# Dividing attention outputs two steps later in a fused attention and expert kernel

## The chip, the cores and the metric

The kernel runs on one core of a Trainium2 chip. The metric is device time in microseconds (us) of one execution. The engines are TensorE (PE, whose weight loads the profile counts apart as PEld), VectorE (DVE), ScalarE (ACT), GpSimd (POOL) and SyncE (SP), which here only issues DMA transfers. Every engine works through its own queue in order.

## The reference, cut to what matters

The input x is 8 batches of 1024 tokens with 256 features, in float32. A transformer block is computed: self-attention with 16 heads of 16 features, a relative position bias that is multiplied by a gate per query, then a residual and a layernorm, then a mixture of 8 experts (two per token, capacity 2560 rows, a fallback network for what overflows), again with a residual and a layernorm. What matters for the change is the attention:

```python
gate_out = gate_a * (gate_b * gru_const - 1.0) + 2.0
gated_bias = gate_out * pos_bias[None]
scores = jnp.einsum('bhid,bhjd->bhij', q, k) * scale + gated_bias
attn = jax.nn.softmax(scores, axis=-1)
out = jnp.einsum('bhij,bhjd->bhid', attn, v)
```

The kernel does not normalise `attn`. It multiplies exp(scores) by v with a column of ones added to it, so that the sum of each softmax row comes out as one more row of the output, and divides the output by that sum afterwards. This division is what the change moves.

## The kernel before, in words

**Units and steps.** The attention is cut into 64 units: 8 batches times 8 pairs of heads (HP = 2). A unit is 16 steps (STEPS): 8 tiles j of 128 keys times 2 chunks c of 512 queries, step s = 2j + c. The loop at L1309 counts steps as g, with unit u and step s of it; `sb` is the step within a batch's 128. In this document the place of a unit is u mod 8, its place in its batch. The order of work is written out by hand (`manual_schedule`, L393): what is recorded first stands first in its engine's queue.

**One step.** PE multiplies keys and queries of two heads into the PSUM tile `sc` (L1107, two buffers). DVE adds the gated bias `gb` (L1122, in 12 of 16 steps), ACT takes the exponential into `pr` (L1129), and in odd steps PE multiplies four `pr` tiles with v into `o_acc` (L1137). Interleaved with it, 21 steps ahead (LEAD), an upper bound of each query's scores is found: two PE products `pm` (L1023, L1027), a relu on ACT (L1052) and a fold on DVE (L1064). `pm0` has one PSUM bank; in even steps the product takes the common bank instead, if that is free. Before a unit begins, `shift` (L1075) turns these bounds into a row of its queries: a PE transpose `pmr` at step 11 (SHIFT_AT), a copy on ACT (L1083), a DVE operation (L1085), and two DMAs `qs<-row` (L1092), which the first scores of the next unit read.

**POOL** makes the gated bias of a tile every second step (`gate_biases`, L983, two tiles ahead, four buffers, from `bias` and `gates`), a diagonal `dgb` (L996), and the small operations of the streams.

**The end of a unit.** `take_outputs` (L1146) works in the steps of the next unit: ACT copies `o_acc` into `osb` at step 1 (L1149); at step 2 four DMAs take the rows of sums to 128 partitions (`sums<-osb`, L1154); at step 4 DVE takes reciprocals (L1170); at step 5 four DMAs take them back (`recs<-sums`, L1164). Then `divide` (L1173), at step DIVIDE_AT: PE spreads the reciprocals over the partitions (`pb<-recs,sel`, L1177, two matmul records), in the step after it DVE multiplies `osb` by `pb` (L1181), and four DMAs store it (`oD<-osb`, L1191). `sums`, `recs` and `osb` have one buffer each.

**SP's queue in a unit.** Step 1: two loads of `biasb`. 2: four `sums`. 3 and 4: twelve loads of `ks` and `ks_d` for the unit after next. 5: four `recs`. 6: seven loads of `qs`. 8: `bias`. 9: `gates` of the next unit's tiles 0 to 2 (L965). Then four `oD`. 13: two `qs<-row`. 15: the other `gates`. Among them, up to about unit 23, stands every fourth step one transfer that clears `xd` or `yd` (L402).

**Streams.** What a batch's neighbours need runs beside the steps as generators: the prologue (projections) of the next batch, the epilogue (output projection `po`, layernorm, routing) of the batch before, and then 16 scatters of rows (`xd<-xt`, L888) on POOL, one in each odd step. All of them, and `divide` and `shift`, share one PSUM bank (`ps_x`). A user of it is held to its last read (HELD: read by ACT, SLOW: read by DVE, a step later); `Streams.bank` gives the bank to the list `own` (`divide`, `shift`) first, then to the streams in turn. In step 10, the step ahead of the shift, streams get no bank (`others`, L1356). The streams of a batch begin at `sb == 12`, in its first unit; the epilogue reads `oD`, which the last division of the batch before has to have stored.

After the units come the epilogue of the last batch and the expert stage (L1378 to L1565), which the diff does not touch.

## Time and profile before

| what | value |
|---|---|
| median of 3 runs | 3706.02 us (3704.2 to 3713.74) |
| the profiled execution's own time | 3705.5 us |
| its span | 3703.8 us |
| PE busy | 3293.6 us (89%) |
| PEld busy | 1663.7 us (45%) |
| POOL busy | 2221.0 us (60%) |
| ACT busy | 2045.0 us (55%) |
| DVE busy | 1944.0 us (52%) |
| first scores of unit 0, last scores of unit 63 | 147.7 us, 2522.0 us from the span's start |
| mean unit of batches 1 to 6, places 0 to 7 | 35.9, 44.4, 41.4, 43.6, 38.6, 32.9, 33.2, 33.2 us |

The busy shares are means over the whole span, expert stage included. The last row is read from the starts of the scores' matmuls (L1107): units at places 1 to 3 carry most of the streams' PE work, units at places 4 to 7 and 0 little of it.

### The profile page before, as it was taken

How to read it: one execution, taken by the hardware profiler on the slowest of the kernel's cores; microseconds unless marked ns; L12 is line 12 of the kernel's file. 1: busy time of each engine (PE TensorE's matmuls, PEld its weight loads, DVE VectorE, ACT ScalarE, POOL GpSimd, SP SyncE). 2: the span in 40 equal slices, each digit the busy share in tenths (PEclk: the TensorE clock that was granted, in tenths of full speed). 3: DMA queues.
4: the chain of work that ended last, by engine and by line, in shares of the span. 5: the costliest groups of instructions: out<-in, count | busy, mean ns of one | idle time of the engine just before them, and what ended most of it. 6: DMA issues, size and time to landing. Idle time of an engine off the chain costs nothing. (4 is left out here: it accounts for less than half of the span.)

```text
span 3703.8 us, 53431 instructions
## 1 busy us (share of the span) xinstructions
PE 3293.6 (89%) x16263; PEld 1663.7 (45%) x16263; DVE 1944.0 (52%) x5559; ACT 2045.0 (55%) x3084; POOL 2221.0 (60%) x2619
## 2 busy tenths in 40 slices
PE   4798898999899999999999999995299999999998
PEld 2242243334334334334333433332176667677776
DVE  2455566665756656665666576662033444344443
ACT  1576776777767777777777777772022222222222
POOL 2566666876886787787787688683333333333332
PEclk8899999999999999999999999996599999999999
DMA  5566666565543444444434444430322321332220
GB/s 133 153 167 192 167 172 183 173 195 181 179 140 110 144 135 122 134 136 122 139 123 141 133 123 128 129 111 15 107 70 74 90 87 54 92 94 94 71 89 22
DMA packets 380594, 455.71 MB, mean 123 GB/s; under 512 B 87653, under 2 KB 285410, under 8 KB 380282
## 3 DMA queue, kind: packets, MB, share of 16 engines
q1 hardware_dynamic: 338602, 388.06, 35.5%
q0 software_dynamic: 19296, 43.38, 4.1%
q10 hardware_dynamic: 22384, 20.58, 1.9%
q8 instruction: 138, 2.26, 0.3%
q14 instruction: 174, 1.43, 0.1%
HBM read 315.16 MB, written 140.54 MB: 123 GB/s over the span
## 5 line engine op out<-in xcount | busy, mean ns | idle before, releaser
L1129 ACT ACTIVATE pr<-sc 128x1024 f32<-128x1024 f32 x1024 | 1046.8, 1023 | 303.7 <-DVE sc L1122 297.9
L983 POOL TENSOR_TENSOR gb<-bias,gates 128x1024 f32<-128x1024 f32 (+2 forms) x512 | 1070.5, 2091 | 190.1 <-DMA gates<-gd 114.3
L1064 DVE CUSTOM_DVE_ANT_0 over<-pm,over 128x512 f32<-128x512 f32 x1024 | 704.3, 688 | 884.7 <-ACT over L1052 281.3
L1052 ACT ACTIVATE over<-pm 128x512 f32<-128x512 f32 x1024 | 609.3, 595 | 344.0 <-PE pm L1027 327.2
L1107 PE MATMUL sc<-qs,ks 122*128 122x512 bf16 x2048 | 625.1, 386 | 26.3 <-ACT pr L1129 18.5
L1122 DVE TENSOR_TENSOR sc<-sc,gb 128x640 f32<-128x640 f32 (+3 forms) x768 | 599.6, 781 | 46.6 <-POOL gb L983 21.0
L1027 PE MATMUL pm<-biasb,dgb 128*128 128x320 bf16 (+2 forms) x2048 | 581.7, 284 | 17.2 <-POOL dgb L996 17.2
L1137 PE MATMUL o_acc<-pr,v 128*17 128x512 f32 x4096 | 562.5, 621 | 0.3 <-ACT pr L1129 0.3
L1474 PE MATMUL ph<-xsT,w 128*128 128x512 f32 (+1 forms) x1440 | 487.6, 497 | 13.0 <-ACT xsT L1414 13.0
L1489 PE MATMUL py<-w,hT 128*128 128x256 f32 x2208 | 485.0, 379 | 5.9 <-DVE ys L1496 5.9
L1489 PEld LDWEIGHTS py<-w,hT 128*128 128x128 f32 x2208 | 419.2, 190 | 74.5 <-issue 10.5
L1023 PE MATMUL pm<-ks,qs 120*128 120x512 bf16 x1024 | 397.8, 388 | 57.3 <-DVE mh L1064 33.9
L1023 PE MATMUL pm<-ks_d,qs 120*128 120x512 bf16 x1024 | 397.1, 388 | 25.0 <-ACT over L1052 13.6
L1023 PEld LDWEIGHTS <-qs 120*128 120x128 bf16 x2048 | 208.9, 102 | 467.4 <-issue 303.4
L1481 ACT ACTIVATE hT<-ph,b_sb 128x512 f32<-128x512 f32 (+1 forms) x360 | 211.6, 588 | 287.3 <-PE ph L1474 286.3
L1474 PEld LDWEIGHTS ph<-xsT,w 128*128 128x128 f32 x1440 | 270.2, 190 | 212.7 <-issue 166.5
L1414 ACT COPY xsT<-pt 128x512 f32<-128x512 f32 (+1 forms) x90 | 39.5, 489 | 566.9 <-PE pt L1411 472.8
L143 POOL TENSOR_TENSOR rs<-rstd,neghalf 128x1 f32<-128x1 f32 x138 | 78.2, 566 | 442.2 <-DVE rstd L141 441.8
L1027 PEld LDWEIGHTS <-dgb 128*128 128x128 bf16 x2048 | 202.4, 99 | 301.6 <-issue 161.8
L996 POOL TENSOR_TENSOR dgb<-anti,grev 128x256 bf16<-128x256 f32 x512 | 314.2, 614 | 4.6
L1107 PEld LDWEIGHTS <-ks 122*128 122x128 bf16 x2048 | 199.8, 100 | 202.0 <-issue 52.3
L419 POOL TENSOR_TENSOR parts<-rest,parts 128x512 bf16<-128x512 f32 (+1 forms) x80 | 92.6, 1158 | 267.0 <-ACT parts L418 201.6
(184 smaller groups left out, 2929.7 us busy)
## 6 DMA issues: line engine op xcount, KB each, us to landing
gates<-gd SPq DMA_DIRECT2D x64, 832.0 KB
biasb<-stripb SPq DMA_DIRECT2D x128, 288.0 KB
gates<-gd SPq DMA_DIRECT2D x64, 576.0 KB
bias<-blocks SPq DMA_DIRECT2D x64, 512.0 KB
xd<-zero SPq DMA_DIRECT2D x51, 522.0 KB
ks<-kd SPq DMA_DIRECT2D x384, 64.0 KB
qs<-qd SPq DMA_DIRECT2D x384, 64.0 KB
yd<-zero SPq DMA_DIRECT2D x40, 512.0 KB
```

What stands on the lines that cost most here:

```text
L983: nc.gpsimd.tensor_tensor(gb_[:, :, off : off + hi - lo], me.bias[:, :, off : off + hi - lo], gates[:, :, lo - at : hi - at], ALU.mult,)
L996: nc.gpsimd.tensor_tensor(dg, anti.unsqueeze(1).to_broadcast([P, HP, P]), batches[b].grev[:, i, hp * HP : (hp + 1) * HP] .unsqueeze(2) .to ...
L1023: nc.tensor.matmul(pm, QS[u % 3][:R_SHIFT, h, i * P : (i + 1) * P], keys, start=True, stop=False)
L1027: nc.tensor.matmul(pm[:, lo:hi, :], dgb[m - h][:, h, :], me.biasb[:, at : at + (hi - lo) * P].rearrange("p (j n) -> p j n", n=P)[:, :, :HALF],
L1052: nc.scalar.activation(me.over, pm, AF.Relu)
L1064: nc.vector.tensor_tensor_reduce(out=me.over, in0=me.rest, in1=me.over, scale=1.0, scalar=-3.0e38, op0=ALU.add, op1=ALU.max, accum_out=me. ...
L1107: nc.tensor.matmul(me.sc[:, h, :], ks[:, h, j * P : (j + 1) * P], qs[:, h, c * CH : (c + 1) * CH], start=True, stop=True,)
L1122: nc.vector.tensor_tensor(sc[:, :, lo - c * CH : hi - c * CH], sc[:, :, lo - c * CH : hi - c * CH], me.gb[j][:, :, off : off + hi - lo], A ...
L1129: nc.scalar.activation(pr, sc, AF.Exp)
L1137: nc.tensor.matmul(o_acc[r : r + D + 1, :], batches[b].v[:, j, hp * HP + h, :], prs[c][:, h, :], start=(j == 0), stop=(j == NI - 1),)
L1474: nc.tensor.matmul(ph[:, :size], w1_sb[:, k, f * P : (f + 1) * P], xsT[:, k, :size], start=(k == 0), stop=(k == NK - 1),)
L1489: nc.tensor.matmul(py, hT[:, f, t * P : (t + 1) * P], w2_sb[:, f, :], start=(f == 0), stop=(f == NF - 1),)
```

## The change

The step of the division goes from 8 to 10, and the streams of a batch's neighbours start at `sb == 14` instead of 12. Nothing else differs. The amount of work is the same, instruction for instruction; their order in the queues is not.

```diff
@@ -44,7 +44,7 @@
 LEAD = 21
 SHIFT_AT = -LEAD % 16
-DIVIDE_AT = 8
+DIVIDE_AT = 10
 EPS = 1e-5
@@ -1312,7 +1312,7 @@
             m = g + LEAD
             if g < G:
-                if sb == 12:
+                if sb == 14:
                     assert not streams.of or streams.of[0][0].__name__ == "scatters"
```

What that does to the order, as the changed program's queues have it:

- At places 0 and 4 to 7, `pb` stands in step 10 instead of 8, `osb<-osb,pb` and the four `oD` transfers in step 11 instead of 9. The product `pm` of step 8 takes the common bank and that of step 10 the bank `pm0` (before, the other way round), at the places where the bank was free at all. `pmr` stays in step 11.
- At place 1, `pb` goes from step 9 to 11, and `pmr` from 11 to 12, after that step's `pm`; `qs<-row` is issued in step 14 instead of 13. At places 2 and 3, `pb` comes in step 10.
- The streams start in step 14 of place 0 and stand one step later at places 0 and 1. From step 13 of place 2 they stand where they did: step 8 is now free for them. The scatters do not move.
- After unit 63, `pb` comes at step 10 of the empty steps instead of 8.

## Prediction

> **What bounds the kernel now.** I read the page first, then PE's waits, then the timelines of single units. PE is busy for 9 tenths of nearly every slice of the attention stage, and the units' lengths follow PE's work, so a wait of PE is worth time there. The list of PE's waits begins so (waiting line, releaser, us in all, times, longest):

> ```profile
> PE pb L1177 <- DMA recs<-sums: 74.6, 29, 8.3
> PE pt L1411 <- DMA xs<-xd: 60.7, 1, 60.7
> PE pm L1023 <- DVE mh L1064: 33.9, 56, 2.1
> ```

> The reader sees that the largest wait of PE is the division's: `pb` stands in PE's queue before its reciprocals have come back. The 8.3 us is the division after unit 63, where nothing else is left; it stays. 66.3 us lie inside the units.

> Why they come late is in SP's timeline of unit 15 (start, us, line; its step 0 begins at 720.27):

> ```profile
> 725.05 2.44 SPq L1154 DMA_DIRECT2D sums<-osb  x4
> 727.59 2.85 SPq L915 DMA_DIRECT2D ks<-kd  x6
> 730.49 2.76 SPq L915 DMA_DIRECT2D ks_d<-dd  x6
> 733.29 0.42 SPq L402 DMA_DIRECT2D yd<-zero  x1
> 733.82 2.76 SPq L1164 DMA_DIRECT2D recs<-sums  x4
> ```

> `recs` is issued behind twelve loads, back to back since `osb` was ready, and lands 1.3 us after 736.57. This is SP's time from the unit's start, not PE's. PE's timeline of the same unit:

> ```profile
> 734.62 0.38 PE L1023 MATMUL pm<-ks_d,qs 120*128 120x512 bf16 x1
> 734.84 0.27 PE L1027 MATMUL pm<-biasb,dgb 128*128 128x256 bf16 x1
> 737.86 1.09 PE L1177 MATMUL pb<-recs,sel 4*128 4x512 f32 x2 [2.75 <-DMA recs<-sums]
> ...
> 739.85 0.63 PE L1023 MATMUL pm<-ks_d,qs 120*128 120x512 bf16 x1
> 740.27 0.36 PE L1027 MATMUL pm<-biasb,dgb 128*128 128x192 bf16 x1
> 740.57 1.91 PE L1137 MATMUL o_acc<-pr,v 128*17 128x512 f32 x8
> ```

> PE waits 2.75 us, and 2 us later the same product takes 0.63 instead of 0.38 us. The table of stretches (us, PE busy, PEld, DVE, ACT, POOL, granted clock, DMA) says why:

> ```profile
> 734.20:737.90 3.70, 0.95 (x7) 0.35 (x4) 1.18 (x3) 2.49 (x3) 3.62 (x4) 1.00 0.58 189
> 737.90:739.40 1.50, 1.50 (x5) 0.53 (x6) 0.00 (x0) 0.00 (x0) 1.26 (x3) 1.00 0.53 167
> 739.40:742.90 3.50, 3.50 (x14) 0.65 (x13) 2.04 (x4) 1.62 (x2) 3.31 (x4) 0.51 0.54 128
> ```

> The granted clock falls to half for some 3.4 us. Of 31 such waits above 0.5 us, 24 are followed by that: 17 stretches of 3.41 us and 7 of 6.83, 105.8 us at half clock. PE is busy in nearly all of it, so they cost 51.2 us beside the 66.3.

> **The change part by part.** *Removed.* A pair of steps at places 4 to 7 takes 1.15 + 2.29 = 3.44 us where nothing waits (median of steps 0 and 1 of place 7), so `pb` two steps later asks for `recs` 3.44 us later. All but four waits are shorter (unit 4 has 4.87; units 6, 7 and 23 3.6 to 3.8), and those four lose nearly all too. Available is 66.3 + 51.2 = 117.5 us, little less for the rests.

> *What is late next: POOL.* At places 6 (end), 7 and 0 POOL scatters rows. Its timeline in unit 31:

> ```profile
> 1334.06 0.62 POOL L996 TENSOR_TENSOR dgb<-anti,grev 128x256 bf16<-128x256 f32 x1
> 1334.85 1.01 POOL L888 DMA_INDIRECT xd<-xt,slot_i  x1 [0.17 <-issue]
> 1335.88 2.38 POOL L983 TENSOR_TENSOR gb<-bias,gates 128x1024 f32<-128x1024 f32 x1
> 1338.21 0.61 POOL L996 TENSOR_TENSOR dgb<-anti,grev 128x256 bf16<-128x256 f32 x1
> 1338.99 1.01 POOL L888 DMA_INDIRECT xd<-xt,slot_i  x1 [0.17 <-issue]
> ```

> One scatter to the next is 4.14 us: POOL needs 4.14 us for the two steps that PE does in 3.44. The 16 scatters of this batch run from 1330.61 to 1396.6, and no gap in that time waits for PE. So here PE's wait is time in which POOL catches up. The lead of a tile (end of its `gb` on POOL to the DVE add that reads it) shows it: 5.4 us for the second tile of unit 31, down to 3.3 at tile 4, back to 6.9 at tile 5 after the wait; in unit 32 down to 1.2, and 6.8 after its wait. Where a lead is used up, a saved wait turns into a wait of the DVE add for `gb`; PE feels it about a us later, having two `sc` buffers (my estimate, between 0 and a step pair's 3.4).

> The account for units 29 to 32: available 2.5, 3.7, 3.9 and 5.8, in all 15.9. POOL last waits for the loaded gates in unit 30, at a time set by that unit's start, so 2.5 moves POOL too and counts in full. Of the 3.7 + 3.9 saved after it, tile 4 of unit 32 lets through its lead of 1.2 and 1: 2.2. With 5.8 that is 8.0, of which the first tile of unit 33 (lead 6.2) lets through 7.2. Kept: 9.7, with small gaps of POOL 10.1. The same by batch, available and kept, each taken from its unit 2 to the second unit of the next: 31.2 and 31.2 (no scatters yet), 13.6 and 4.3 (unit 16 has leads of 0), 17.5 and 9.3, 15.9 and 10.1, 9.0 and 4.5, 11.5 and 5.8, 11.1 and 4.8, 7.7 and 7.7 (none left). Kept in all: **77.7 us**; 71 with no us of PE's own, 90 with three.

> *Moved: `pb` and the multiply.* 64 times 1.09 and 0.68 us, the same work, now in steps 10 and 11. `pmr` follows on the one bank: from `pb`'s start to the multiply's end is 2.28 + 0.68 = 2.96 us (unit 31), and PE has 1.02 (`pb`) + 0.34 (`pm`) + 0.91 (scores, `pm`) + 0.99 (`o_acc`) = 3.26 us of work before `pmr`. It costs nothing as long as DVE is no later than that; if late by a fold (0.69) at 38 units, 26 us. At place 1 `pmr` is nearer, 1.02 + 0.34 + 0.91 + 0.34 = 2.61 us: 0.35 us at 8 units, 3 us. I take 3.

> *Moved: four `oD` transfers on SP*, past a clearing transfer to just ahead of `qs<-row`. They are 2.4 to 3.5 us of issue. Behind them wait `qs<-row`, `gates` and the next `biasb`. `qs<-row` now ends its issue 3.9 us ahead of the next unit, held by the DVE row (4.5 ahead), not by SP. After it, `pb` starts some 10.5 us ahead of a light unit's end, and `oD` is through 5.5 us later (unit 31: 17.1 to 22.6 from its start), 5.0 ahead, when the row is not ready yet. In the early units with clearing transfers SP itself is later: unit 15's `gates` are issued 22.1 us after its start; 3.5 for `oD`, 0.6 for a clearing transfer and 1.2 for the row make 27.4, and 1.3 to land 28.7, of a unit of some 29.5 us. I take 0, and keep the other end as a rival. Gates are issued ahead of them: not later.

> *Moved: streams.* Their PE work is the same, and from step 13 of place 2 their place too. Place 1 is PE's (42.8 busy of 44.4 us): 0. The first `po` now follows the `oD` issue by 3 steps instead of 4. PE's two waits of `po` for `oD` are 1.7 us in all; at 7 batches the bound is one odd step less, 7 x 2.3 = 16 us, at best 0; I take 0, as the margin is still some 0.7 us.

> Sum: 3705.5 - 77.7 + 3 = **3631 us**. The profiled execution is 0.5 us below the median shown, which changes nothing.

> **The rivals.**

> *All is kept.* If PE passes over POOL's late tiles, 3705.5 - 117.5 = 3588. For it: unit 40 has three tiles with leads of 0.3 and less, and DVE's waits for `gb` are 21.0 us in all. Against it: unit 16, leads 0 throughout, took 36.0 us with a wait of only 0.7 at `pb`.

> *The clock does not come back.* If the halves at steps 8 to 11 are only shifted, or new ones start where PE waits for POOL, the waits alone count: 66.3, of which by the same account 53.0 is kept: 3653. For it: 8 of the 32 half-clock stretches of the units follow no wait for `recs`; against it: 24 do. [...]

> *The shift row becomes the wait (slower).* PE's scores at a unit's start read `qs<-row`; today 4 waits, 6.9 us. If DVE and SP run later than I worked out, each us past the remaining 0.8 to 2 costs 38 units a us plus a half-clock stretch's 1.7. At 1.5 us: 38 x 3.2 = 122, less 75: 3753. It decides from 2.0 us a unit on. Against it: SP idles 6 us a unit ahead of `sums` (752.0 to 758.1).

> *It does nothing:* `recs` drifts with the queue and `pb` waits as before, 3700. Against it: SP starts anew at `osb` in each unit.

> **How the numbers follow.** Forecast, with 3610 to 3645 around it: 0.53. All kept 0.14, clock stays 0.18, nothing 0.07, slower 0.08. A measurement of this kernel tells about 0.3% (11 us) from no change: faster 0.85, same 0.07, slower 0.08. The range leaves out the last two: from just under 3588 to 3653 and a further 25 for the bank (26 us): 3585 to 3678.

> **What would show it.** PE's wait of `pb` for `recs` falls from 74.6 to about 10 us, nearly all after unit 63. Half-clock stretches in the units fall from 32 to about 10. Place 5 shortens by some 3 us; place 0 little, and DVE's waits of `sc` for `gb` grow from 21 to 50 us or more. Wrong would be: `sc` waiting for `qs<-row` by tens of us, `pmr` for `osb`, or `gb` waits unchanged with places 7 and 0 shorter by 4 us each.

## The result, and the profile after

| | before | after |
|---|---|---|
| median of 6 runs each on one chip, us | 3709.11 (3704.2 to 3713.74) | 3674.59 (3668.03 to 3679.04) |
| ratio, 95% interval | 1 | 0.9907 (0.9894 to 0.992) |
| the profiled execution, and its span, us | 3705.5, 3703.8 | 3676.38, 3674.6 |
| stage: first scores of unit 0 to last scores of unit 63, us | 2374.3 | 2341.4 |
| PE busy, idle in the stage, us | 2191.0, 183.3 | 2180.7, 160.7 |
| stretches at half clock in the stage, PE's loss in them, us | 32, 65.7 | 21, 40.3 |
| mean unit of batches 1 to 6, places 0 to 7, us | 35.8 44.4 41.4 43.6 38.6 32.9 33.2 33.2 | 36.3 45.7 42.7 43.8 36.9 31.7 31.2 30.7 |

The change makes the kernel 34.5 us faster, where 74.7 us were forecast; the stage of the units has 32.9 of it. The loss in the last row but one is an estimate: half of PE's busy time in the stretches at half clock, where a product `o_acc` takes 1.05 us on average against 0.60 at the full clock, in both traces. By place, places 4 to 7 gain (48.9 us over all batches, from the starts of the scores), and places 0 to 2 give 17.9 us back.

PE's waits in the kernel after (the columns are as in the prediction):

```profile
PE pt L1411 <- DMA xs<-xd: 61.4, 1, 61.4
PE sc L1107 <- ACT pr L1129: 32.5, 29, 3.5
...
PE pm L1023 <- DMA qs<-qd: 25.8, 18, 8.2
...
PE pb L1177 <- DMA recs<-sums: 12.3, 5, 8.9
```

The wait that headed the list is gone: 74.6 us in 29 waits became 12.3 in 5, of which 8.9 is the division after unit 63. But the product `pm` now waits for `qs<-qd` 18 times. Before, that was one wait, ahead of the units:

```profile
PE pm L1023 <- DMA qs<-qd: 8.3, 1, 8.3
```

In the kernel after, 17.6 of the 25.8 us lie in the units, 17.5 of them in step 11. And `sc` waits longer for ACT (18.5 us before), which stands behind DVE. Why is in DVE's list, first before and then after:

```profile
DVE sc L1122 <- POOL gb L983: 21.0, 18, 2.9
DVE sc L1122 <- POOL gb L983: 80.9, 54, 4.5
```

POOL's tiles come later relative to PE, as was expected. A third group has grown that no single line shows. PE's waits at the streams' own products (every product of PE but `sc`, `pm`, `pb`, `pmr` and `o_acc`) sum to 11.1 us of the stage before and to 36.5 after, most of it at places 1 and 2. One of its lines, before and after:

```profile
PE pq L620 <- ACT x1T L732: 2.5, 6, 0.4
PE pq L620 <- ACT x1T L732: 7.3, 12, 1.0
```

The new wait at work, in unit 15, the unit that the prediction showed. First SP's timeline of the kernel after (the unit starts at 707.13):

```profile
720.68 2.74 SPq L1164 DMA_DIRECT2D recs<-sums  x4
723.46 0.55 SPq L907 DMA_DIRECT2D qs<-fd  x1
724.06 3.84 SPq L915 DMA_DIRECT2D qs<-qd  x6
```

Then PE's timeline of the same time:

```profile
726.55 1.12 PE L1177 MATMUL pb<-recs,sel 4*128 4x512 f32 x2
...
729.93 0.38 PE L1023 MATMUL pm<-ks_d,qs 120*128 120x512 bf16 x1 [1.42 <-DMA qs<-qd]
730.14 0.25 PE L1027 MATMUL pm<-biasb,dgb 128*128 128x192 bf16 x1
730.32 1.05 PE L1137 MATMUL o_acc<-pr,v 128*17 128x512 f32 x8
```

`recs` is issued 13.55 us after the unit's start, as before to the hundredth; `pb` now stands late enough and does not wait. Behind `recs` in SP's queue stand the seven loads of `qs` for the unit after next. The bounds run 21 steps ahead, so in step 11 PE reads that `qs` for the first time: 1.42 us too early here. Before the change PE got there after its wait for `recs`, which covered this one.

### The profile page after: what moved, and what is told of

Read it like the earlier page. It is cut to its first block, busy times and chain, and to the rows that moved or that the text cites. A ratio compares the mean times of both kernels' runs of the same rounds, so it can differ in the third digit from the quotient of the medians.

```text
span 3674.6 us, 53450 instructions
## 1 busy us (share of the span) xinstructions
PE 3285.5 (89%) x16263; PEld 1656.9 (45%) x16263; DVE 1930.6 (53%) x5559; ACT 2045.6 (56%) x3084; POOL 2223.5 (61%) x2619
## 3 DMA queue, kind: packets, MB, share of 16 engines
q14 instruction: 173, 1.42, 0.1%
## 5 line engine op out<-in xcount | busy, mean ns | idle before, releaser
L983 POOL TENSOR_TENSOR gb<-bias,gates 128x1024 f32<-128x1024 f32 (+2 forms) x512 | 1071.5, 2093 | 178.0 <-DMA gates<-gd 102.6
L1064 DVE CUSTOM_DVE_ANT_0 over<-pm,over 128x512 f32<-128x512 f32 x1024 | 703.7, 687 | 815.0 <-ACT over L1052 302.4
L1107 PE MATMUL sc<-qs,ks 122*128 122x512 bf16 x2048 | 619.3, 383 | 42.8 <-ACT pr L1129 32.5
L1122 DVE TENSOR_TENSOR sc<-sc,gb 128x640 f32<-128x640 f32 (+3 forms) x768 | 599.7, 781 | 94.2 <-POOL gb L983 80.9
L1027 PE MATMUL pm<-biasb,dgb 128*128 128x320 bf16 (+2 forms) x2048 | 577.9, 282 | 16.7 <-POOL dgb L996 16.7
L1137 PE MATMUL o_acc<-pr,v 128*17 128x512 f32 x4096 | 553.9, 612 | 0.3 <-ACT pr L1129 0.3
L1023 PE MATMUL pm<-ks,qs 120*128 120x512 bf16 x1024 | 396.1, 387 | 43.8 <-DVE mh L1064 25.1
L1023 PEld LDWEIGHTS <-qs 120*128 120x128 bf16 x2048 | 207.3, 101 | 502.6 <-issue 334.7
L1023 PE MATMUL pm<-ks_d,qs 120*128 120x512 bf16 x1024 | 392.9, 384 | 39.2 <-DMA qs<-qd 25.7
L1027 PEld LDWEIGHTS <-dgb 128*128 128x128 bf16 x2048 | 201.7, 98 | 278.9 <-issue 147.5
L996 POOL TENSOR_TENSOR dgb<-anti,grev 128x256 bf16<-128x256 f32 x512 | 315.1, 616 | 4.9
L1509 POOL DMA_INDIRECT out_dram<-o,dst_i x138 | 145.3, 1053 | 158.1 <-DVE o L145 69.5
```

The lines of the kernel that those rows point to most:

```text
L983: nc.gpsimd.tensor_tensor(gb_[:, :, off : off + hi - lo], me.bias[:, :, off : off + hi - lo], gates[:, :, lo - at : hi - at], ALU.mult,)
L996: nc.gpsimd.tensor_tensor(dg, anti.unsqueeze(1).to_broadcast([P, HP, P]), batches[b].grev[:, i, hp * HP : (hp + 1) * HP] .unsqueeze(2) .to ...
L1023: nc.tensor.matmul(pm, QS[u % 3][:R_SHIFT, h, i * P : (i + 1) * P], keys, start=True, stop=False)
L1027: nc.tensor.matmul(pm[:, lo:hi, :], dgb[m - h][:, h, :], me.biasb[:, at : at + (hi - lo) * P].rearrange("p (j n) -> p j n", n=P)[:, :, :HALF],
L1064: nc.vector.tensor_tensor_reduce(out=me.over, in0=me.rest, in1=me.over, scale=1.0, scalar=-3.0e38, op0=ALU.add, op1=ALU.max, accum_out=me. ...
L1107: nc.tensor.matmul(me.sc[:, h, :], ks[:, h, j * P : (j + 1) * P], qs[:, h, c * CH : (c + 1) * CH], start=True, stop=True,)
```

## The experiments

Stage spans are of one profiled execution each, from the first to the last scores; "gap" is PE idle in the stage and "loss" the estimate of what half clock costs it. Medians and ratios are of whole kernels, beside the kernel before on the same chip; the last column has the median of the kernel before there. Chips differ by up to 0.4% and executions of one kernel on one chip by some 5 us either way, so a difference of two stages is good to some 7 us on one chip, and to about 10 us across chips (my estimate from these times). Ratios are safer where there are any.

| kernel | median, us | ratio (95%) | stage | gap | loss | before there |
|---|---|---|---|---|---|---|
| before | | 1 | 2374.3 | 183.3 | 65.7 | 3709.11 |
| after | 3674.59 | 0.9907 (0.9894 to 0.992) | 2341.4 | 160.7 | 40.3 | 3709.11 |
| qs_early | 3658.74 | 0.9863 (0.9846 to 0.9879) | 2320.9 | 149.6 | 31.8 | 3709.27 |
| loads_early | 3635.81 | 0.9796 (0.9778 to 0.9814) | 2301.1 | 136.1 | 20.0 | 3709.27 |
| loads_early_8 | 3635.82 | 0.9768 (0.9752 to 0.9784) | 2296.6 | 140.6 | 20.0 | 3722.75 |
| streams_only | 3727.57 | 1.0053 (1.0033 to 1.0072) | 2390.3 | 187.2 | 71.4 | 3709.27 |
| prologue_12 | 3712.49 | 1.0009 (0.9993 to 1.0024) | 2388.3 | 186.8 | 57.4 | 3709.27 |
| no_scatter_8 | | | 2382.0 | 193.9 | 63.7 | 3722.75 |
| no_scatter_10 | | | 2320.0 | 148.2 | 41.9 | 3722.75 |
| early_no_scatter | | | 2298.3 | 135.5 | 27.7 | 3722.75 |
| early_8_no_scatter | | | 2268.0 | 117.6 | 20.8 | 3712.03 (one run) |
| wide_pb_10 | 3679.37 | 0.9886 (0.9865 to 0.9908) | 2347.6 | 190.9 | 26.5 | 3721.83 |
| wide_pb_8 | 3695.68 | 0.9938 (0.9914 to 0.9962) | 2359.5 | 199.7 | 35.5 | 3721.83 |

The theory after the result: the wait for `recs` had two followers, the scatters of POOL, which were counted, and the loads of `qs` behind it in the same queue, which were not. The rival: POOL alone took the gain back.

### qs_early and loads_early: the queue behind recs

The changed kernel, with the seven loads of `qs` in step 0, so that they are ahead of `recs`:

```diff
-                    for which, at_ in enumerate((3, 4, 6)):
+                    for which, at_ in enumerate((3, 4, 0)):
```

> The changed kernel with one line more: the seven loads of qs for the unit after next go from step 6 to step 0, into the time in which SP waits for osb. Theory (qs is late next): in the changed kernel PE waits in step 11 for qs<-qd, 17.3 us in 15 places, and the clock halves that begin there cost 25.8 us. Both vanish, recs is no later, and the time falls by 43 us less what POOL takes of it: 3635 to 3655 us. Rival (POOL alone took the gain; the wait in step 11 only covers its lateness): 3675 us, within 6, with the waits of the DVE add for gb growing from 81 us by what the wait for qs loses.

Measured: 3658.74 us, and the stage 20.5 us shorter. The waits for `qs` in the units fall from 17.6 us to 0, and step 11 summed over units 1 to 62 from 191 to 162 us. The half-clock loss falls only from 40.3 to 31.8; 15.4 of that still lies in step 11. It comes between the two expectations, nearer to the theory; by the ratios it gains 16 us over the kernel after. SP's queue is shorter here at the gates too: those of the first tiles are issued 17.0 and 17.7 us after a unit's start at places 7 and 0, instead of 20.3 and 21.6 (batch 0 left out), and DVE's waits for `gb` fall from 80.9 to 45.9 us. So the run moves two things, `qs` and the gates.

Then the twelve loads of `ks` and `ks_d` ahead of `recs` instead, in steps 1 and 0, so that `recs` is issued as soon as its reciprocals are there, and `qs` comes after it, but early:

```diff
-                    for which, at_ in enumerate((3, 4, 6)):
+                    for which, at_ in enumerate((1, 0, 6)):
```

> The changed kernel with the twelve loads of ks_d and ks at steps 0 and 1 instead of 4 and 3; qs stays at step 6. SP's wait of some 6 us for osb takes 5.6 us of issue, so recs and qs are issued up to 5 us earlier in the unit. Theory (qs is late next): as with qs early, 3635 to 3655 us, step 11 near 2.3 us at places 5 to 7. Rival (POOL alone): 3675 us, within 6. If the early loads delay sums, recs comes no earlier and pb waits again: above 3680.

Measured: 3635.81 us, at the lower edge of the theory's range, with the stage 40.3 us shorter than that of the kernel after (41 us by the ratios). Summed over all units, step 11 gives 34.5 us of it and step 3 of place 0, where PE follows POOL, 13.3; the other steps together give 7.5 back. The gates of the first tiles are issued 17.1 and 18.3 us after a unit's start at places 7 and 0, and DVE's waits for `gb` fall to 45.0 us.

So the order of SP's queue cost the kernel after some 40 us. `qs` and the gates do not explain all of it: qs_early has no waits for `qs` either, gates as early and as little waiting for `gb`, and gains half. Of the 19.8 us between the two stages, place 0 has 12.5. There POOL's own queue shows a wait that the prediction did not count: a scatter waits until an earlier scatter has landed. In unit 16 of the kernel after, PE's longest wait for ACT stands behind one:

```profile
747.10 1.01 POOL L888 DMA_INDIRECT xd<-xt,slot_i  x1 [3.92 <-DMA xd<-xt,slot_i]
750.26 1.10 DVE L1122 TENSOR_TENSOR sc<-sc,gb 128x896 f32<-128x896 f32 x1 [4.44 <-POOL gb L983]
752.53 1.01 PE L1107 MATMUL sc<-qs,ks 122*128 122x512 bf16 x2 [3.54 <-ACT pr L1129]
```

In steps 2 to 4 of place 0 these waits of POOL sum to 17.0 us in the kernel after, to 12.7 in qs_early and to 1.4 in loads_early, where they stand in step 1 instead. That fits, but no run changed them alone, so this share stays open.

### loads_early_8: is the later step worth anything by itself?

The same early loads in the kernel before, with the division in step 8 and the streams at 12.

> The kernel before (division in step 8, streams from 12) with ks_d and ks loaded at steps 0 and 1. recs lands some 12 to 13 us after the unit's start, before step 8 (14.7). If the wait for recs was the whole reason for the gain, and the later place of the streams cost some 18 us of it, this is faster than the same loads with the division in step 10 (3636): 3612 to 3630 us. If the division in step 10 has a worth of its own, 3640 or more. If sums are late through the loads ahead of them, pb still waits, over 20 us in all.

Measured: 3635.82 us, ratio 0.9768, the lowest ratio of the kernels that do the whole work; it beats the kernel before and the kernel after. Its timeline of SP in unit 15 (which starts at 693.49):

```profile
698.42 2.44 SPq L1154 DMA_DIRECT2D sums<-osb  x4
700.90 0.58 SPq L402 DMA_DIRECT2D yd<-zero  x1
704.48 2.44 SPq L1164 DMA_DIRECT2D recs<-sums  x4
706.96 0.54 SPq L907 DMA_DIRECT2D qs<-fd  x1
```

Nothing stands between `sums` and `recs` but the time until the reciprocals; `recs` is issued 11.0 us after the unit's start instead of 13.55. From PE's waits, of the same kernel:

```profile
PE pb L1177 <- DMA recs<-sums: 13.6, 2, 8.6
...
PE pm L1023 <- DMA qs<-qd: 10.5, 1, 10.5
```

One wait of 5.0 us is left in the units, at `pb` in step 8. Steps 8 and 9 lose 103 us together (426 to 323, units 1 to 62), and the stage 77.7; by the ratio the kernel gains 86 us. As measured, the time lies between the two expectations, but this chip is slower than that of loads_early: with the ratio, 3709.27 us there would be 3623, inside the first. What follows: once `recs` is early, the later division, with the streams' later start that goes with it, is worth nothing; it costs 4.5 us by the stages and 0.3% by the ratios, whose intervals just overlap.

### streams_only and prologue_12: the streams' later place

The kernel before, with only the start of the streams moved:

```diff
-                if sb == 12:
+                if sb == 14:
```

> The kernel before with the streams at step 14 alone; the division stays in step 8. pb waits for recs as before, 74.6 us. If the streams' place costs nothing, 3709 us, within 8; if it costs what places 0 to 2 lose in the changed kernel, 3727 us.

Measured: ratio 1.0053, stage 16.0 us longer, in size as the second expectation. Its reason does not hold, though. Places 0 to 2 are together 2.8 us shorter than before; the time is lost at place 4, which grows from 38.6 to 41.7 us, and its half-clock loss from 10.0 to 24.6. PE's wait at `pb` stays (75.0 us). In the kernel after, place 4 gets shorter, so these 16.0 us can't be carried over to it. What can is the group of waits at the streams' own products: 25.7 us here against 11.1 before, and 36.5 where the division is later too. In all the kernels of the table with the division in step 8 and the streams at 12 this sum is 11 to 14 us, and in all with step 10 and 14 it is 35 to 43. The later place is not free.

In prologue_12 the prologue begins at 12 and only the epilogue at 14, in the kernel after:

```diff
-                if sb == 14:
+                if sb == 12:
...
-                    if b:
-                        streams.start(epilogue(b - 1, batches[b - 1]))
...
+                if sb == 14 and b:
+                    streams.start(epilogue(b - 1, batches[b - 1]))
```

> The changed kernel, but the prologue of the next batch starts at step 12 of a batch as before; only the epilogue, which reads the last division, starts at 14. In the changed kernel the units at places 0, 1 and 2 are 3, 9 and 5 us longer in all than before. If the streams' later place does that: 3657 us, with places 0 to 2 back to their lengths before. If it is POOL's lateness and pb and pmr in steps 11 and 12 of place 1: 3675 us, within 6.

Measured: ratio 1.0009, neither expectation. The two streams now take the common bank in another order, and `pb` in step 11 with `pmr` in step 12 falls on place 3. Of PE's waits in this kernel:

```profile
PE sc L1107 <- DMA qs<-row: 38.2, 15, 6.3
```

This line is the rival "the shift row becomes the wait", at 38.2 us, against 6.9 before and 6.7 after. It shows that the order of the streams can bring this rival about, but as a test of the streams' start the run says nothing.

### Without the scatters: POOL's share

Four kernels leave out the scatters on POOL (the line `streams.start(scatters(b, xt))`), so the expert stage gets no rows; only their stages are compared. The first is otherwise the kernel before, the second the kernel after:

> The kernel before without the 16 scatters of a batch: the expert stage then gets no rows and writes none, so only the stage from the first to the last scores is compared (2374.3 us before, 2341.4 changed, a difference of 32.9). If POOL's scatters take the gain back only where pb no longer waits, they cost the kernel before little: the stage takes 2360 to 2375 us, and pb still waits for recs by 55 to 75 us in the units.

> The changed kernel without the scatters, compared as no scatter with the division in step 8. Theory (POOL's scatters take some 40 us of the gain): the stage falls by 25 to 40 us from 2341, and the difference of the two kernels without scatters is 55 to 75 us instead of 33; what is still missing to 117 stays with qs in step 11. DVE's waits for gb fall from 81 to under 25 us. Rival (POOL's lateness is covered by PE's buffers and costs nothing): the difference stays within 8 of 33.

Measured: 2382.0 and 2320.0 us. The first is above the 2360 to 2375 expected, and `pb` waits 75.7 us in the units, just above the 55 to 75: without scatters the kernel before got no shorter. Its chip takes 0.4% more for the kernel before, which is about as much as those 7.7 us. The change is worth 62.0 us where POOL has no scatters (both on one chip), and 32.9 where it has: the scatters take some 29 us of it. The second stage is 21.4 us below 2341.4 where 25 to 40 were expected, but across chips; the theory's difference of 55 to 75 holds, the rival's 33 does not. No wait of DVE for `gb` is left in the second, and yet the wait for `qs` is there, and longer:

```profile
PE pm L1022 <- DMA qs<-qd: 33.4, 23, 8.2
```

(One line was taken out above it, so L1022 is L1023 of the others; 25.2 us of it lie in the units.)

The third and fourth have the early loads as well, with the division in step 10 and in step 8:

> The changed kernel with ks_d and ks loaded at steps 0 and 1, and without scatters. If the waits for recs, those for qs and POOL's scatters are the whole account, the stage comes to 2374 - 117 + 18 (the streams' place) = 2275 us, within 12. If something else is short, it stays above 2290.

> The kernel before (division in step 8, streams at 12) with the loads of ks_d in step 0 and of ks in step 1, and without the scatters on POOL, so that the expert stage gets no rows; only the stage from the first to the last scores is compared. It closes the account. The waits for recs and their half-clock stretches are gone and nothing of POOL's can take them back. Theory: the later place of the division and of the streams costs PE some 20 us or more at places 0 to 2 (streams_only cost 16 us of the stage); then the stage is 2271 us (2262 to 2280), that is 27 us below the same kernel with the division in step 10 and the streams at 14 (early_no_scatter, 2298.3). Rival: the later place costs nothing when the loads are early, and the waits and half-clock stretches were simply worth less than the 117.5 us of the forecast: 2290 to 2300, as early_no_scatter.

Measured: 2298.3, which is 23 us above what the theory expected of the third and 21.7 below no_scatter_10 on the same chip, and 2268.0, near the middle of what it expected of the fourth. The fourth is a single run on another chip, where the kernel before took 0.3% less, so that some 7 of the 30.3 us between the two may be the chip's. They lie at the later places of the division and the streams: steps 10 and 11 sum to 83 us more and steps 8 and 9 to 58 less, and by place, places 1 to 3 lose 28.7 us together. PE's waits at the streams' products are 35.5 us in the third and 11.2 in the fourth.

### wide_pb_10 and wide_pb_8: what halves the clock

Nine of the 21 stretches left in the kernel after follow a window without a wait of over 0.6 us. All stretches, in every trace of this case, begin on a grid of 3.413 us; in those before and after, all changes of the granted clock (78 and 54) lie within 5 ns of it. In unit 12 of the kernel after, two windows of that grid (the columns are those of the prediction's table of stretches):

```profile
628.50:631.91 3.41, 2.65 (x10) 0.86 (x8) 3.30 (x10) 1.88 (x3) 3.41 (x7) 1.00 0.98 333
631.91:635.32 3.41, 3.41 (x15) 0.88 (x14) 2.33 (x5) 2.21 (x4) 0.13 (x1) 0.50 1.08 240
```

PE is busy for 78% of the first, and the clock granted in the second is 0.50. In PE's timeline the first has

```profile
629.25 1.12 PE L1177 MATMUL pb<-recs,sel 4*128 4x512 f32 x2 [0.48 <-DVE mh L1064]
```

and without this product, whose weights have only 4 rows, PE would be busy for 45%. Over eight traces, 161 of 178 stretches follow a window in which PE was busy for under 48%, if `pb` is not counted, and 14 of the 5077 windows that no half-clock window follows are under that line; with `pb` counted it meets 90 of 178. (With the other three traces of the table that have a `pb` of 4 rows, it is 203 of 232.) So `pb` was given 128 rows, 124 of them zero, with the same instructions in the steps:

```diff
-        sel = cst.tile([4, 4, 32], F32, name="sel")
+        sel = cst.tile([P, 4, 32], F32, name="sel")
+        recs0 = cst.tile([P, CH], F32, name="recs")
+        nc.gpsimd.memset(recs0, 0.0)
...
-                me.recs = rt.tile([4, CH], F32, tag="recs", name=f"recs{u}")
+                me.recs = recs0
```

> The changed kernel, with the product pb over 128 rows instead of 4: sel and recs get 124 more partitions, all zero, and the instructions, their order and their columns stay as they are. Theory: all half-clock stretches start on a grid of 3.413 us, where PE was busy for under some 0.48 of the window before, if the 1.1 us of pb (4 rows) count as idle; so counted, 161 of 178 stretches in eight traces are met, and 14 of 5077 other windows; with pb counted as busy 90 are met. Then a pb of 128 rows counts as busy, and of 21 stretches those whose window is then above 0.48 go: 7 to 10 remain, the half-clock loss falls from 40 to 13 to 20 us, step 11's from 26 to under 8, and the kernel gains 10 to 25 us: 3650 to 3665. Rival: the clock follows PE's gaps whatever the number of rows: 18 or more stretches remain, and 3668 to 3680.

> The kernel before, with the same wide pb. Theory: here most of the stretches follow a wait for recs, with pb right behind it; with pb counted as busy some 20 of 32 windows are still under 0.48, so 18 to 24 stretches remain and the half-clock loss falls from 66 to 40 to 50 us; 3685 to 3700. The division in step 10 is then worth as much as before or a little less, 25 to 40 us between the two wide kernels. Rival: 28 or more stretches remain, 3700 to 3712.

Measured, the clock: 14 stretches instead of 21 (the theory had 7 to 10, the rival 18 or more), and 19 instead of 32, as expected; the loss of the stretches that begin in step 11 falls from 25.8 to 3.4 us in the changed kernel. The same place of unit 12 in wide_pb_10, first its windows and then its `pb` (lines stand two lower there):

```profile
634.15:637.57 3.42, 2.67 (x11) 0.88 (x8) 3.31 (x10) 1.84 (x3) 3.42 (x7) 1.00 1.11 283
637.57:640.98 3.41, 3.11 (x21) 1.12 (x20) 2.91 (x9) 2.38 (x5) 0.15 (x1) 1.00 0.87 210
```

```profile
634.94 1.12 PE L1179 MATMUL pb<-recs,sel 128*128 128x512 f32 x2 [0.48 <-DVE mh L1066]
```

The wait ahead of `pb` (0.48 us) and the busy time (2.67 us against 2.65) are all but the same, and the clock stays at 1.00: the chief difference that these lines show in PE's work is the rows of the product. With `pb` counted, a line at 43% now parts halved windows from the others in wide_pb_10 with one miss.

Measured, the time: wide_pb_8 gains 0.6%, as its theory had it. The two wide kernels, on one chip, are 16 us apart, where 25 to 40 were expected: wide_pb_10 is only 0.2%, 8 us, below the kernel after (ratios 0.9886 and 0.9907, whose intervals overlap), against the 10 to 25 of its theory; its 3679.37 us lie where the rival had them. So the lower loss is not all time won: in wide_pb_8 it falls by 30.2 us, and the kernel gains 23 by its ratio (14.8 by the stage, across chips); in wide_pb_10 it falls by 13.8, and no gain over the kernel after is clear of the noise. In the trace of wide_pb_10 PE's gaps are 30.2 us longer: `sc` for `qs<-row` 6.7 to 20.2, `pm` for `qs<-qd` 17.6 to 21.9, together 17.8 of it. Perhaps PE comes sooner to the same transfers; how much of this is the other chip is not known.

## Why the prediction was right and wrong

**The mechanism was right, as far as it went.** The waits for `recs` went (66.3 to 3.4 us in the units), and DVE's waits for `gb` rose past 50 us, to 80.9. "All is kept" and "It does nothing" are out. What failed is the account of what comes in the place of those waits. The prediction had 53.0 of the 66.3 us kept, so 13.3 lost to POOL. Of PE's waits in the stage, `sc` for ACT, behind POOL, grew by 14.0 us, about as forecast. But `pm` for `qs<-qd` grew by 17.6 and the waits at the streams' products by 25.4, and the forecast had nothing for either.

**Available, 117.5 us: about right.** Without scatters, and with nothing moved later, taking the waits away is worth 2382.0 - 2268.0 = 114.0 us of the stage, by one run and across chips. There was somewhat more to take: 75.7 us of waits at `pb`, and 53.6 of loss in the stretches that begin in steps 8 and 9.

**POOL: about right.** The forecast had POOL take 117.5 - 77.7 = 39.8. With early loads it takes 114.0 - 77.7 = 36.3 (28 if the 86 us of the ratio stand for the 77.7), in the changed kernel 62.0 - 32.9 = 29.1. That the 77.7 of loads_early_8 equals the forecast to the tenth is luck: by the ratio it is 86, and POOL gets its gates there 2 to 3 us earlier.

**The step that failed is "What is late next: POOL".** It named one follower of the removed wait, and there were at least two. The prediction read SP's queue for what is moved in it, `oD`, and for what stands behind that. It did not read it for what stands right behind `recs` and comes to PE after `pb`: the `qs` that step 11 reads. In unit 15 before, `recs` ends its issue at 736.58, and seven more issues behind it take some 4 us; PE two steps later is there first. The table of PE's waits could not show it, since the larger wait covered it. Issuing `qs` ahead of `recs` brings 20.5 us of the stage, 16 by the ratios (qs_early, which brings the gates forward too); early loads bring 21.7 where POOL has no scatters. Taking the twelve loads out of the way brings 40.3 in the kernel as it is (loads_early); what the second half of that is stays open.

**The second step that failed is "Moved: streams ... 0", "Place 1 is PE's: 0" above all.** Places 0 to 2 grew by 17.9 us in the kernel after, places 1 and 2 by 14.6 of it, and PE's waits at the streams' products by 25.4, of which the streams' start alone brings 14.6 (streams_only). Division and streams together cost 30.3 us without scatters, by one run across chips. With scatters and early loads the two kernels are 4.5 us apart, 10 by the ratios; perhaps PE stands before POOL's tiles there anyway, which was not tested. On the path over the two kernels with early loads the stages read -77.7 + 4.5 + 40.3 = -32.9, by the ratios -86 + 10 + 41 = -35, and without scatters -114.0 + 30.3 + 21.7 = -62.0. Such sums close by construction; the terms change with the order in which they are taken.

**The clock: half right.** Stretches at half clock were to fall to about 10 and fell to 21. The loss fell by 25.4 us, which is what the forecast's own sum had kept of the 51.2 (77.7 - 53.0 = 24.7), so in the sum this term was not off; its count of 10 did not go with it. The rival that the clock does not come back was right in part: 15 of the 21 stretches begin in steps 10 and 11, so they are shifted there, and three begin in step 3 (units 16, 40 and 63) during a wait of 3.1 to 3.5 us for ACT, behind POOL. Nine of the 15 lie at places 2 to 4, after waits of 0.6 us at most: the moved `pb` now shares a window with PE's small pauses there. In unit 12 the clock was at half after a window (628.50 to 631.91) whose longest wait was 0.48 us, beside a 4-row product.

**The small terms.** `oD` on SP: 0 was right, `sc` for `qs<-row` stays at 6.7 us, and the shift row did not become the wait in the changed kernel. `po` for `oD`: 1.4 us, right. The gates of the first tiles are issued 20.3 us after the start of a unit at place 7 against 20.6, but 21.6 against 20.4 at place 0: "not later" holds but for that 1.2 us. `pmr`, 3 us: its waits changed their releaser (for `mh` before, for `osb` and `sc` now) more than their sum; too small to judge. Place 0 hardly moved (0.5 us a unit), right; place 5 lost 1.2 us instead of 3.

## What to carry to other kernels

Before pricing a wait that goes, follow the queue of the transfer it waited for, and write down when each transfer behind it lands and who reads it next: a large wait hides every smaller one in its wake. Compare moving the consumer later with issuing the transfer earlier; here the second, one line, won more than twice as much (2.3% against 0.9%) and left the division and the streams in their places. Gains of two covers do not add: take each away alone and both together before naming a share.
